# Third weight combination of a modulated four-layer convolution: 18 block products in place of 19, three of them shared

## The chip, the cores and the metric

One core of a Trainium2 chip, float32 throughout. The metric is the device time of one execution in microseconds (us). The kernel before was run three times; the profile is of one execution on the same kind of chip. Engines: PE (TensorE), DVE (VectorE), ACT (ScalarE), POOL (GpSimd), SP (DMA issue).

## The reference

128 samples, each with 64 channels of 1024 positions, go through four convolutions of three taps whose weights are modulated for each sample by a style vector; the result is added to the input.

```python
TYPES = ('same', 'upsample', 'same', 'downsample')
def _layer(x, style, w, b, mw, mb, typ):
    s = style @ mw.T + mb
    weight = SCALE * w * s[:, None, :, None]
    demod = lax.rsqrt(jnp.sum(weight * weight, axis=(2, 3)) + EPS)
    weight = weight * demod[:, :, None, None]
    if typ == 'same':         # stride 1, padding 1
        out = jax.vmap(_conv_same)(x, weight) + b[None, :, None]
    elif typ == 'upsample':   # transposed, stride 2, then blur
        out = jax.vmap(_conv_up)(x, weight.transpose(0, 2, 1, 3)) + b[None, :, None]
        out = _blur(out, 2.0 * blur_k, (1, 1))
    elif typ == 'downsample': # blur, then stride 2
        out = jax.vmap(_conv_down)(_blur(x, blur_k, (2, 2)), weight) + b[None, :, None]
    return out
return x + _L0_cond_ref(x, cond_512, ...)
```

Everything is linear, so the four layers of a sample can be merged into one filter of nine taps of 64x64, and only that filter is run over the sample.

## The kernel before

The samples are taken four at a time, in NQ = 32 groups q. PE is used as four quarters of 64x64, so that one product of a weight block with the four samples is a group of four matmuls: `r` is the row half and PSUM bank, `c` the column half. A four-byte matmul leaves two records in the trace.

**Making the filter** of a group takes four steps. `scale3` scales the last layer's weights into `wd` (ACT). `stage1_a` and `stage1_b` multiply by the third layer's weights into the PSUM tile `psS`; ACT evicts the first part as S after `stage1_a`, and `stage1_b` goes on adding into the same bank, from which DVE makes the sums (L442). `stage2` multiplies by the second layer merged with the blur (`E`) into `psR`; part of its products is shared (`share` into a free part of `psA`, `share_copy` into `psR`). ACT evicts it, scaled by `tC`, as R: seven blocks of 64 columns for each half. The **third combination**, `stage3`, multiplies R by the first layer's three taps w0, w1, w2. The filter's block j (0 to 8) is the sum over k of tap k times R block j - k. ACT evicts the nine blocks, scaled by `t0`, as `Wf`.

In the steady turns stage3 is split. `stage3_b` puts 12 blocks of products, in seven groups of matmuls, into the new group's `psA` bank: five finished filter blocks, and two products shared by two blocks each, which use sums of R blocks (`r_sums`, L588, two slots of R). ACT copies these shared ones into `psW` with the factors 1 and 1/3 (L609). `stage3_a` adds seven more blocks in four groups to `psW`, and ACT evicts four filter blocks from there. The taps j = 0, 3, 6 / 1, 4, 7 / 2, 5, 8 need the scales 1, 1/3 and -2 for what follows; they are in the weights (`w0s`), and the blocks lie in `Wf` in an order set by `TAPS`. `psS`, `psR` and `psW` share the one pair of banks of the pool `ps_w`.

**Running the filter.** Positions are split into three planes. Five products (`conv0` to `conv4`; each three groups of matmuls of 340 columns, L753) of sums of the taps (`combine_a`, `combine_b` on DVE, tile H) with sums of the planes give three outputs. DVE and POOL make the plane sums: `in_g01`, `in_g2` (tile G), `in3` (L711, DVE, into T3), `in04` (L740, DVE), and `in1` and `in2` (L726 and L731, on POOL in the steady turns). conv3, conv1, conv2 and conv0 add up in `psA`; `copy_m3` (ACT), `sum1` and `sum2` (DVE) take values out between them. `sum2` writes Y = 3 m3 - psA into the PSUM tile Y (two instructions, L662), then updates y1 (L812), and `conv4` adds its product into that Y. ACT makes the outputs (L830), SP stores them and loads the next planes.

**Order.** The schedule is written out by hand; every engine runs its instructions in the order of the program. A steady turn (`turn_of`, q = 5 to 28; q = 4 is an entry with a somewhat other order) handles output of group q, the convolutions of n = q + 1, the filter of c = q + 2 and stage1 of s = q + 4:

```python
stage2(c); conv2(q); r_sums(c, nc_g); sum2(q); in2(n, nc_g)
stage3_b(c, open_a(n)); combine_a(n); conv4(q); stage3_a(c)
combine_b(n); conv3(n); outputs(q, 2); stage1_a(s); copy_m3(n)
in04(n); share_sums(c + 1); in_g2(c); conv0(q, 0, 1, 2)
outputs(q, 1); stage1_b(s); in_g01(c); share(c + 1); share_copy(c + 1)
outputs(q, 0); conv1(n); sum1(n); in3(c); in1(c, nc_g); scale3(s + 1)
```

In q = 10, 14, 15 and 19 PE also does small matmuls for the samples' ends before conv1. Turns before q = 4 and after q = 28 use `stage3`, all 21 products.

Of the kernel before, what the change touches and what calls it, by code (L numbers as in the profile page):

```python
# [48 lines left out]
F32 = mybir.dt.float32  # L49
# [5 lines left out]
C = 64  # L55
K = 3
# [7 lines left out]
def kernel(  # L64
# [199 lines left out]
    def var_newton(bs, ls=slice(0, NL)):  # L264
# [2 lines left out]


    ALT, ODD, DOWN = slice(0, 4, 2), slice(1, 4, 2), (slice(3, 4), slice(1, 2))
    tA, tB, tBn, tC, t0, t3, td, tb = (  # L270
        const.tile([P, NQ, 2], F32, name=n) for n in ("tA", "tB", "tBn", "tC", "t0", "t3", "td", "tb")
    )

    def table(eng, t, bs, upper, lower, src, mul):
# [80 lines left out]
    Wq = {}  # L355
    chain = {}

    def scaled_copy(eng, dst, src, f):
        if eng is nc_a:
            nc_a.activation(dst, src, AF.Copy, scale=f)  # L360
        else:
            eng.tensor_scalar(dst, src, f, None, op0=ALU.mult)
# [39 lines left out]
    def flat(t):  # L402
        return t.rearrange("c a o -> c (a o)")
# [18 lines left out]
    def stage1_a(q, ps=None):  # L422

        ps = ps or unit(ps_w, f"psS{q}")
        wd = chain[q]
        tap_matmul(ps, wd, 2, 2, w2n[:, 0, :], EVEN, first=True)
        tap_matmul(ps, wd, 3, 2, w2n[:, 2, :], EVEN)
        tap_matmul(ps, wd, 1, 1, w2n[:, 1, :], slice(1, 2))
        st, t = s_tiles(q)
        for r in range(2):  # L430
            scaled_copy(nc_a, flat(st[r][:, :4]), ps[r][:, C : 5 * C], tBn[:, q, r : r + 1])
        chain[q] = wd, ps, st, t

    def stage1_b(q):

        wd, ps, st, t = chain[q]
        tap_matmul(ps, wd, 2, 1, w2n[:, 3, :], slice(3, 4))
        tap_matmul(ps, wd, 4, 1, w2n[:, 4, :], slice(4, 5), last=True)
        for r in range(2):
            p1 = st[r][:, 0:1, :].to_broadcast([P, 2, C])  # L440
            sums = ps[r][:, 2 * C : 6 * C].rearrange("c (a b o) -> c a b o", a=2, b=2)[:, :, 0]
# [43 lines left out]
    def share_copy(q):  # L485

        ps = unit(ps_w, f"psR{q}")
        for r in range(2):
            src = shared_ps[q][r].rearrange("c (a o) -> c a o", a=2)
            nc_a.copy(  # L490
                ps[r][:, C : 5 * C].rearrange("c (a b o) -> c a b o", a=2, b=2),
                src[:, :, None, :].to_broadcast([P, 2, 2, C]),
            )
        shared_ps[q] = ps

    def stage2_rest(q):

        ps = shared_ps.pop(q)
        block = lambda i, n=1: [b[:, i * C : (i + n) * C] for b in ps]
        apart = [b[:, : 4 * C].rearrange("c (a b o) -> c a b o", a=2, b=2)[:, :, 0] for b in ps]  # L500
# [16 lines left out]
        for n, (dst, weight, slots) in enumerate(plan):  # L517
            chain_matmul(dst, weight, chain[q], slots, n == len(plan) - 1)
        return ps

    def stage2(q, pool=None, engs=(nc_a, nc_a), between=None):
        st = chain[q]
        shared = q in shared_ps
        ps = stage2_rest(q) if shared else unit(pool or ps_w, f"psR{q}")
        for n, e in enumerate(() if shared else (-2, -1, 0, 1, 2, 3, 4, 5, 6)):
            if e % 2 == 0:
                a, lo, m = slice(1, 4), e // 2 + 1, 3
            else:
# [31 lines left out]

    def tap_shares():
        nc_g.tensor_sub(Wd[:, 0], woi[0][:, 0, :], woi[0][:, 1, :])
        nc_g.tensor_sub(Wd[:, 1], w0s[1][:, 2, :], w0s[1][:, 1, :])

    def blocks(ps, at):
        return [b.rearrange("c (a o) -> c a o", o=C)[:, at, :] for b in ps]
# [10 lines left out]
                    skip_group_check=True,  # L577
                )

    def stage3_out(q, ps, at, n, engs=(nc_a, nc_a)):  # L580
        W = Wq[q][0]
        for r in range(2):
            src = ps[r][:, : n * C].rearrange("c (a o) -> c a o", o=C)
            scaled_copy(engs[r], W[:, at : at + n, r], src, t0[:, q, r : r + 1])

    def r_sums(q, eng):
        t = chain[q]
        eng.tensor_add(t[:, :, 7:9], t[:, :, 2:6:3], t[:, :, 3:7:3])  # L588

    shared_w = {}  # L590

    def stage3_b(q, ps):

        new_w(q)
        t = chain[q]
        plan = (
            (slice(0, 3), w0s[2][:, 2, :], slice(0, 7, 3)),
            (slice(0, 2), w0s[2][:, 1, :], slice(1, 5, 3)),
            (slice(0, 2), w0s[2][:, 0, :], slice(2, 6, 3)),
            (slice(3, 4), w0s[0][:, 0, :], slice(0, 1)),  # L600
            (slice(4, 5), w0s[1][:, 0, :], slice(1, 2)),
            (slice(4, 5), w0s[1][:, 1, :], slice(0, 1)),
            (slice(5, 7), w0s[0][:, 1, :], slice(7, 9)),
        )
        for i, (at, weight, slots) in enumerate(plan):
            same_row(blocks(ps, at), weight, t, slots, i == 0, i == len(plan) - 1)
        pw = shared_w[q] = unit(ps_w, f"psW{q}")
        src = blocks(ps, slice(5, 7))
        for i, f in enumerate((1.0, 1.0 / 3.0)):  # L609
            for dst, v in zip(blocks(pw, slice(i, i + 3, 2)), src):  # L610
                scaled_copy(nc_a, dst, v, f)
        stage3_out(q, ps, 0, 5)

    def stage3_a(q):

        t, pw = chain[q], shared_w.pop(q)
        plan = (
            (slice(0, 3, 2), Wd[:, 0], slice(3, 7, 3)),
            (slice(0, 3, 2), w0s[0][:, 2, :], slice(1, 5, 3)),
            (slice(1, 4, 2), Wd[:, 1], slice(2, 6, 3)),  # L620
            (slice(1, 2), w0s[1][:, 0, :], slice(4, 5)),
        )
        for i, (at, weight, slots) in enumerate(plan):
            same_row(blocks(pw, at), weight, t, slots, last=i == len(plan) - 1)
        stage3_out(q, pw, 5, 4)

    def stage3(q, part, pool=None, engs=(nc_a, nc_a)):

# [6 lines left out]
        for i, kind in enumerate(kinds):  # L635
            for k in range(K):
# [610 lines left out]
    def layers(i, j):  # L1247
# [166 lines left out]
    def turn_of(q):  # L1414
# [222 lines left out]
```

## Time and profile before

| | |
|---|---|
| runs of the kernel before | 479.64, 479.15, 478.75 us; median 479.15 |
| span of the profiled execution | 478.0 us |
| granted TensorE clock, mean | 0.997 |
| DVE, 128x340 into Y (L662) | 64 instructions, mean 517 ns |
| POOL, r_sums (L588) | 24 instructions, mean 737 ns |
| POOL, in1 and in2 (L726, L731) | 28 instructions each, mean 1659 and 1660 ns |
| ACT, evictions and copies of the third combination in the steady turns | 100 of 128 columns, mean 269 ns; 50 of 320, 556 ns; 50 of 256, 470 ns |

The span runs from the first to the last instruction of one profiled execution; no other time of that execution was taken. In rows of a timeline the first number is the start in us from the span's start and the second the time from the first start to the last end of the instructions merged in the row (x2: two of them). "[0.76 <-PE psA L753]" says that the engine sat idle for 0.76 us before, until something that PE wrote to psA at line 753. In rows of groups the numbers behind the bar are busy us in all, mean ns of one, and idle us before them.

### The profile page before, as it was taken

The numbers are of one execution on the slowest core, as the hardware profiler recorded it, in microseconds if no ns is written. First come the engines' busy times: TensorE is split into PE (matmuls) and PEld (weight loads), VectorE is DVE, ScalarE is ACT, GpSimd is POOL, SyncE is SP. The second block draws the span as 40 slices with busy tenths as digits, with TensorE's granted clock in tenths as the row PEclk, the third lists the DMA queues.
The fourth block names the chain that finished last, engine by engine and source line by source line (L and its number), as shares of the span: only waits on it lengthen the run. The fifth ranks groups of instructions, "written<-read, shape, count | busy, mean of one in ns | idle before, by whom it ended". The sixth has DMA issues, their size and how long they took to land.

```text
span 478.0 us, 26721 instructions
## 1 busy us (share of the span) xinstructions
PE 469.6 (98%) x11928; PEld 346.4 (72%) x11928; DVE 417.5 (87%) x690; ACT 310.1 (65%) x708; POOL 163.5 (34%) x197
## 2 busy tenths in 40 slices
PE   8999999999999999999999999999999999999995
PEld 7877788777878876677776677766887777766652
DVE  5889998879889998899979899979989999999895
ACT  5565666667666676666667666667666768766352
POOL 3434032663335342243432233422434432333200
PEclk9999999999999999999999999999999999999998
DMA  5406365544445554345543455533455554445125
GB/s 175 158 28 200 114 195 192 150 139 144 139 150 157 173 173 127 122 151 160 171 149 120 131 170 152 173 127 126 145 169 162 162 154 146 152 146 170 61 91 191
DMA packets 50514, 70.70 MB, mean 148 GB/s; under 512 B 5664, under 2 KB 47328, under 8 KB 50400
## 3 DMA queue, kind: packets, MB, share of 16 engines
q1 hardware_dynamic: 49808, 68.32, 45.8%
q8 instruction: 93, 1.52, 1.5%
q10 hardware_dynamic: 592, 0.69, 0.5%
q14 instruction: 21, 0.17, 0.1%
HBM read 35.36 MB, written 33.62 MB: 144 GB/s over the span
## 4 chain that ended last, share of the span: by engine, by line
PE 95%; DVE 4%; issue 0%; ACT 0%; ACTq 0%; DVEq 0%
PE psA L753 45%; PE Y L753 11%; PE psR L467 9%; PE psA L571 7%; PE psW L571 7%; PE psS L389 6%; PE psR L533 4%; PE psA L467 2%; PE Y L994 2%; DVE H L662 1%; PE Y L180 1%; PE Y L336 1%; DVE G L662 0%; PE psM L204 0%; DVE o L832 0%
## 5 line engine op out<-in xcount | busy, mean ns | idle before, releaser
L753 PE MATMUL psA<-T,H 64*64 64x340 f32 x2304 | 187.3, 447 | 0.8 <-DVE y L662 0.7
L753 PEld LDWEIGHTS psA<-T,H 64*64 64x64 f32 x2304 | 89.9, 133 | 50.0 <-issue 3.1
L662 DVE SCALAR_TENSOR_TENSOR G<-X 128x1376 f32<-128x1376 f32 (+2 forms) x65 | 78.1, 1207 | 1.1 <-DMA X<-in_x 0.9
L726 POOL TENSOR_TENSOR T<-G 128x684 f32<-128x684 f32 x28 | 46.5, 1659 | 73.1 <-DVE G L662 73.1
L445 POOL TENSOR_TENSOR S<-S 128x128 f32<-128x128 f32 x28 | 22.1, 790 | 144.1 <-ACT S L360 136.8
L360 ACT ACTIVATE R<-psR,tC 128x448 f32<-128x448 f32 x63 | 36.5, 630 | 46.3 <-PE psR L467 26.7
L753 PE MATMUL psA<-T,Wf 64*64 64x340 f32 x768 | 63.9, 446 | 0.0
L753 PE MATMUL Y<-T,Wf 64*64 64x340 f32 x768 | 62.8, 451 | 0.1
L662 DVE SCALAR_TENSOR_TENSOR Y<-m,psA 128x340 f32<-128x340 f32 x64 | 33.1, 517 | 28.0 <-PE psA L753 26.6
L360 ACT ACTIVATE psW<-psA 128x128 f32<-128x128 f32 x100 | 19.3, 269 | 50.3 <-PE psA L571 46.2
L740 DVE TENSOR_TENSOR T<-G 128x1368 f32<-128x1368 f32 (+1 forms) x33 | 50.7, 1540 | 0.0
L360 ACT ACTIVATE Wf<-psW,t 128x256 f32<-128x256 f32 (+2 forms) x76 | 32.7, 479 | 26.5 <-PE psW L571 26.2
L711 DVE TENSOR_TENSOR T<-X 128x684 f32<-128x684 f32 x32 | 47.9, 1496 | 0.0
L467 PE MATMUL psR<-S,E 64*64 64x64 f32 (+1 forms) x1472 | 46.5, 238 | 0.0
L731 POOL TENSOR_TENSOR T<-G 128x684 f32<-128x684 f32 x28 | 46.5, 1660 | 0.0
L389 PEld LDWEIGHTS psS<-wd,w2n 64*64 64x64 f32 x1120 | 35.0, 133 | 13.3 <-ACT S L360 0.8
L467 PEld LDWEIGHTS psR<-S,E 64*64 64x64 f32 x1472 | 39.6, 134 | 5.2 <-ACT psR L490 0.2
L753 PEld LDWEIGHTS Y<-T,Wf 64*64 64x64 f32 x768 | 29.6, 132 | 18.0 <-DVE Y L662 0.7
L830 ACT ACTIVATE o<-psA,tb,td 128x340 f32<-128x340 f32 x63 | 37.0, 647 | 6.3 <-PE psA L753 6.3
L753 PEld LDWEIGHTS psA<-T,Wf 64*64 64x64 f32 x768 | 29.1, 133 | 15.1
L830 ACT ACTIVATE o<-Y,tb,td 128x340 f32<-128x340 f32 x63 | 36.6, 637 | 4.5 <-PE Y L753 2.7
L830 ACT ACTIVATE o<-y,tb,td 128x340 f32<-128x340 f32 x62 | 38.5, 679 | 0.6 <-DVE y L812 0.6
(165 smaller groups left out, 832.4 us busy)
## 6 DMA issues: line engine op xcount, KB each, us to landing
out<-o SPq DMA_DIRECT2D x167, 170.0 KB, 2.6
X<-in_x SPq DMA_DIRECT2D x150, 172.0 KB, 3.6
X<-in_x SPq DMA_DIRECT2D x14, 516.0 KB, 5.3
out<-o SPq DMA_DIRECT2D x6, 510.0 KB, 5.4
out<-o SPq DMA_DIRECT2D x2, 340.0 KB, 3.0
Xe<-in_x_ends SPq DMA_DIRECT2D x1, 512.0 KB, 6.7
out<-o ACTq DMA_DIRECT2D x3, 170.0 KB, 2.3
par<-in_params SPq DMA_DIRECT2D x2, 192.0 KB, 3.4
```

The source lines that it names most:

```text
L360: nc_a.activation(dst, src, AF.Copy, scale=f)
L389: nc.tensor.matmul(ps[r][cols, at * C : (at + n) * C], weight[rows], wd[c if r == 0 else 1 - c][rows, taps], start=first, stop=last, skip_ ...
L445: nc_g.tensor_add(t[:, :, 2], t[:, :, 2], t[:, :, 0])
L467: nc.tensor.matmul(dst[r][cols], weight[rows], st[c if r == 0 else 1 - c][rows, slots, :], start=False, stop=last, skip_group_check=True,)
L571: nc.tensor.matmul(dst[r][cols], weight[rows], t[rows, c, slots, :], start=first, stop=last, skip_group_check=True,)
L662: nc_v.scalar_tensor_tensor(out, x, f, y, op0=ALU.mult, op1=op)
L711: nc_v.tensor_sub(t[:, pairs, 0, :NJ], plane(X, 3, pairs), plane(X, 1, pairs))
L726: eng.tensor_add(t[:, :, 0, :NJ], plane(g, 2), plane(g, 1))
L731: eng.tensor_sub(t[:, :, 1, :NJ], plane(g, 2), plane(g, 1))
L740: nc_v.tensor_sub(t[:, pairs, :, :NJ], both(a, PL), both(b, 1))
L753: nc.tensor.matmul(ps[s][cols, :NB], w, Ts[q, tag][rows, c, i, g : g + NB], start=(g == 0 and m == 3), stop=(g == K - 1), skip_group_check ...
L830: nc_a.activation(dst, src, AF.Identity, bias=add, scale=d3)
```

## The change

The third combination is rearranged into 18 blocks of products in eight groups.

- `stage3_b` now makes six blocks in four groups: filter blocks 7 and 8 whole (three products), and three shared ones, w1 times R0+R1, R2+R3 and R4+R5. `r_sums` makes three slots of sums in place of two, and **does so on DVE in every turn** (before: on POOL, but for the entry turn).
- ACT copies each shared block twice, unscaled, into blocks 1 to 6 of `psW` (two instructions in place of four).
- `stage3_a` makes the other 12 blocks, in four groups of three, three, four and two blocks, with w0 - w1 and w2 - w1 as weights where a shared product is already there.
- The scales 1, 1/3, -2 of these seven filter blocks move from the weights into the eviction: tables `t0`, `t0b`, `t0c` (two more POOL instructions in turn 3), and two evictions of 256 columns become six, of three, two and two blocks.
- The filter lies in natural order; `psS` and `psR` move up by one block, since `psW` now needs block 0 untouched.
- In the steady turns the first third of `conv0` goes ahead of `stage1_a`, and `copy_m3` ahead of stage1_a's evictions.

On PE, around the third combination of turn q = 17, the kernel before has conv2 (psA_4979), stage3_b (psA_5249), conv4 (Y) and the start of stage3_a (psW):

```order
L753 MATMUL psA_4979<-T_17_4891,H_4694 64x340 x12
L571 MATMUL psA_5249<-R_5223,w0s_154 64x192 x4
L571 MATMUL psA_5249<-R_5223,w0s_154 64x128 x8
L571 MATMUL psA_5249<-R_5223,par 64x64 x4
L571 MATMUL psA_5249<-R_5223,w0s_153 64x64 x8
L571 MATMUL psA_5249<-R_5223,par 64x128 x4
L753 MATMUL Y<-T_17_5091,Wf_4693 64x340 x12
L571 MATMUL psW_0_5280<-R_5223,wsq 64x2x64 x2
L571 MATMUL psW_1_5281<-R_5223,wsq 64x2x64 x2
```

The changed kernel has, at the same place on PE (psA_4863 is conv2's tile, psA_5123 the new group's):

```order
L763 MATMUL psA_4863<-T_17_4775,H_4588 64x340 x12
L576 MATMUL psA_5123<-R_5097,w0s_155 64x64 x8
L576 MATMUL psA_5123<-R_5097,w0s_156 64x64 x4
L576 MATMUL psA_5123<-R_5097,par 64x192 x4
L763 MATMUL Y<-T_17_4969,Wf_4587 64x340 x12
L576 MATMUL psW_0_5142<-R_5097,wsq 64x3x64 x2
L576 MATMUL psW_1_5143<-R_5097,wsq 64x3x64 x2
```

Between conv2 and conv4 stand 16 matmuls of 6 blocks where there were 28 of 12; the wide ones are now behind conv4.

On DVE, in the same turn, before: in3 (T_18), the two halves of sum2's Y, y1, and the first of combine_a:

```order
L711 TENSOR_TENSOR T_18_5159<-X_107 128x2x342
L662 SCALAR_TENSOR_TENSOR Y<-m_17_5089,psA_4979 128x340 x2
L812 TENSOR_TENSOR y_17_5157<-y_17_5157,psA_4979 128x680
L662 SCALAR_TENSOR_TENSOR H_4981<-Wf_4980 128x384
L659 SCALAR_TENSOR_TENSOR Wf_4980<-idn_155,t_138,Wf_4980 128x64 x2
```

And on DVE after the change:

```order
L721 TENSOR_TENSOR T_18_5033<-X_107 128x2x342
L597 TENSOR_TENSOR R_5097<-R_5097 128x2x192
L672 SCALAR_TENSOR_TENSOR Y<-m_17_4946,psA_4863 128x340 x2
L822 TENSOR_TENSOR y_17_5031<-y_17_5031,psA_4863 128x680
L672 SCALAR_TENSOR_TENSOR H_4865<-Wf_4864 128x384
```

r_sums (R) has come in between in3 and sum2. On POOL the row of L588 between in1 and in2 is gone, so that in2 stands right behind in1.

On ACT, before: the shared copies into psW, the evictions to Wf, the outputs of Y, stage1_a's evictions S, and copy_m3 (m_18):

```order
L360 ACTIVATE psW_0_5280<-psA_5249 128x2x64
L360 ACTIVATE psW_1_5281<-psA_5249 128x2x64
L360 ACTIVATE psW_0_5280<-psA_5249 128x2x64
L360 ACTIVATE psW_1_5281<-psA_5249 128x2x64
L360 ACTIVATE Wf_5250<-psA_5249,t_137 128x5x64 x2
L360 ACTIVATE Wf_5250<-psW_0_5280,t_137 128x4x64
L360 ACTIVATE Wf_5250<-psW_1_5281,t_137 128x4x64
L830 ACTIVATE o_5337<-Y,tb,td 128x340 x2
L360 ACTIVATE S_5356<-psS_0_5342,tBn 128x256
L360 ACTIVATE S_5356<-psS_1_5343,tBn 128x256
L792 COPY m_18_5359<-psA_5249 128x680
```

And on ACT after the change, from the second copy on:

```order
L617 COPY psW_1_5143<-psA_5123 128x384
L365 ACTIVATE Wf_5124<-psA_5123,t_137 128x2x64 x2
L365 ACTIVATE Wf_5124<-psW_0_5142,t_137 128x3x64
L365 ACTIVATE Wf_5124<-psW_1_5143,t_137 128x3x64
L365 ACTIVATE Wf_5124<-psW_0_5142,t0b 128x2x64
L365 ACTIVATE Wf_5124<-psW_1_5143,t0b 128x2x64
L365 ACTIVATE Wf_5124<-psW_0_5142,t0c 128x2x64
L365 ACTIVATE Wf_5124<-psW_1_5143,t0c 128x2x64
L840 ACTIVATE o_5201<-Y,tb,td 128x340 x2
L802 COPY m_18_5206<-psA_5123 128x680
L365 ACTIVATE S_5226<-psS_0_5212,tBn 128x256
L365 ACTIVATE S_5226<-psS_1_5213,tBn 128x256
```

Behind stage3_a there are six evictions for two, and the m copy has passed the S evictions.

The diff, cut to its core (the shifts of psS and psR by one block are shown once):

```diff
+    def table_0_kinds():
+        for t, f in ((t0b, 1.0 / 3.0), (t0c, -2.0)):
+            nc_g.tensor_scalar_mul(t, t0, f)
...
-            scaled_copy(nc_a, flat(st[r][:, :4]), ps[r][:, C : 5 * C], tBn[:, q, r : r + 1])
+            scaled_copy(nc_a, flat(st[r][:, :4]), ps[r][:, 2 * C : 6 * C], tBn[:, q, r : r + 1])
...
-    TAPS = slice(3, 9, 2), slice(4, 9, 2), slice(0, 3)
+    TAPS = slice(0, 9, 3), slice(1, 9, 3), slice(2, 9, 3)
...
-        nc_g.tensor_sub(Wd[:, 1], w0s[1][:, 2, :], w0s[1][:, 1, :])
+        nc_g.tensor_sub(Wd[:, 1], woi[0][:, 2, :], woi[0][:, 1, :])
...
     def r_sums(q, eng):
         t = chain[q]
-        eng.tensor_add(t[:, :, 7:9], t[:, :, 2:6:3], t[:, :, 3:7:3])
+        eng.tensor_add(t[:, :, 7:10], t[:, :, 0:6:2], t[:, :, 1:7:2])
...
     def stage3_b(q, ps):
...
         plan = (
-            (slice(0, 3), w0s[2][:, 2, :], slice(0, 7, 3)),
-            (slice(0, 2), w0s[2][:, 1, :], slice(1, 5, 3)),
-            (slice(0, 2), w0s[2][:, 0, :], slice(2, 6, 3)),
-            (slice(3, 4), w0s[0][:, 0, :], slice(0, 1)),
-            (slice(4, 5), w0s[1][:, 0, :], slice(1, 2)),
-            (slice(4, 5), w0s[1][:, 1, :], slice(0, 1)),
-            (slice(5, 7), w0s[0][:, 1, :], slice(7, 9)),
+            (slice(3, 4), w0s[1][:, 2, :], slice(5, 6)),
+            (slice(3, 4), w0s[1][:, 1, :], slice(6, 7)),
+            (slice(4, 5), w0s[2][:, 2, :], slice(6, 7)),
+            (slice(0, 3), woi[0][:, 1, :], slice(7, 10)),
         )
...
-        src = blocks(ps, slice(5, 7))
-        for i, f in enumerate((1.0, 1.0 / 3.0)):
-            for dst, v in zip(blocks(pw, slice(i, i + 3, 2)), src):
-                scaled_copy(nc_a, dst, v, f)
-        stage3_out(q, ps, 0, 5)
+        for r in range(2):
+            src = ps[r][:, : K * C].rearrange("c (a o) -> c a o", o=C)
+            dst = pw[r][:, C : 7 * C].rearrange("c (a b o) -> c a b o", b=2, o=C)
+            nc_a.copy(dst, src[:, :, None, :].to_broadcast([P, K, 2, C]))
+        for r, src in enumerate(blocks(ps, slice(3, 5))):
+            scaled_copy(nc_a, Wq[q][0][:, 7:9, r], src, t0[:, q, r : r + 1])
 
     def stage3_a(q):
...
         plan = (
-            (slice(0, 3, 2), Wd[:, 0], slice(3, 7, 3)),
-            (slice(0, 3, 2), w0s[0][:, 2, :], slice(1, 5, 3)),
-            (slice(1, 4, 2), Wd[:, 1], slice(2, 6, 3)),
-            (slice(1, 2), w0s[1][:, 0, :], slice(4, 5)),
+            (slice(1, 6, 2), Wd[:, 0], slice(1, 6, 2)),
+            (slice(2, 7, 2), Wd[:, 1], slice(0, 5, 2)),
+            (slice(0, 7, 2), woi[0][:, 0, :], slice(0, 7, 2)),
+            (slice(3, 6, 2), woi[0][:, 2, :], slice(1, 4, 2)),
         )
...
-        stage3_out(q, pw, 5, 4)
+        for kind, scale in enumerate((t0, t0b, t0c)):
+            at = slice(kind, 7, K)
+            for r, src in enumerate(blocks(pw, at)):
+                scaled_copy(nc_a, Wq[q][0][:, at, r], src, scale[:, q, r : r + 1])
...
             conv2(q)
-            r_sums(c, nc_g)
+            r_sums(c, nc_v)
             sum2(q)
...
         outputs(q, 2)
+        if not entry:
+            copy_m3(n)
+            conv0(q, 0)
         if s < NQ:
             stage1_a(s)
-        if not entry:
-            copy_m3(n)
         in04(n)
...
-        conv0(q, *((2,) if entry else range(K)))
+        conv0(q, *((2,) if entry else (1, 2)))
```

More of the change, by code (lines that the diff above doesn't have):

```diff
@@ L269 @@
     ALT, ODD, DOWN = slice(0, 4, 2), slice(1, 4, 2), (slice(3, 4), slice(1, 2))
-    tA, tB, tBn, tC, t0, t3, td, tb = (
-        const.tile([P, NQ, 2], F32, name=n) for n in ("tA", "tB", "tBn", "tC", "t0", "t3", "td", "tb")
+    tA, tB, tBn, tC, t0, t0b, t0c, t3, td, tb = (
+        const.tile([P, NQ, 2], F32, name=n) for n in ("tA", "tB", "tBn", "tC", "t0", "t0b", "t0c", "t3", "td", "tb")
     )
@@ L436, in stage1_b @@
         wd, ps, st, t = chain[q]
-        tap_matmul(ps, wd, 2, 1, w2n[:, 3, :], slice(3, 4))
-        tap_matmul(ps, wd, 4, 1, w2n[:, 4, :], slice(4, 5), last=True)
+        tap_matmul(ps, wd, 3, 1, w2n[:, 3, :], slice(3, 4))
+        tap_matmul(ps, wd, 5, 1, w2n[:, 4, :], slice(4, 5), last=True)
         for r in range(2):
             p1 = st[r][:, 0:1, :].to_broadcast([P, 2, C])
-            sums = ps[r][:, 2 * C : 6 * C].rearrange("c (a b o) -> c a b o", a=2, b=2)[:, :, 0]
+            sums = ps[r][:, 3 * C : 7 * C].rearrange("c (a b o) -> c a b o", a=2, b=2)[:, :, 0]
             nc_v.scalar_tensor_tensor(
@@ L498, in stage2_rest @@
         ps = shared_ps.pop(q)
-        block = lambda i, n=1: [b[:, i * C : (i + n) * C] for b in ps]
-        apart = [b[:, : 4 * C].rearrange("c (a b o) -> c a b o", a=2, b=2)[:, :, 0] for b in ps]
+        block = lambda i, n=1: [b[:, (i + 1) * C : (i + 1 + n) * C] for b in ps]
+        apart = [b[:, C : 5 * C].rearrange("c (a b o) -> c a b o", a=2, b=2)[:, :, 0] for b in ps]
         plan = (
@@ L650, in stage3 @@
                 )
-        stage3_out(q, ps, *((3, 6), (0, 3))[part], engs)
+        stage3_out(q, ps, kinds, engs)
         return ps
```

29 lines of the change are left out of this document (16 added, 13 removed).

## The prediction

> **What bounds the kernel now.** I read the page first, then TensorE's waits, then one steady turn engine by engine.
>
> ```profile
> span 478.0 us, 26721 instructions
> PE 469.6 (98%) x11928; PEld 346.4 (72%) x11928; DVE 417.5 (87%) x690; ACT 310.1 (65%) x708; POOL 163.5 (34%) x197
> PE 95%; DVE 4%; issue 0%; ACT 0%; ACTq 0%; DVEq 0%
> PE Y L180 <- DVE eps L156: 1.4, 1, 1.4
> PE psA L571 <- issue: 0.8, 2, 0.5
> PE psA L753 <- DVE y L662: 0.7, 1, 0.7
> PE psA L753 <- DVE T L726: 0.2, 1, 0.2
> ```
>
> The busy times and the chain of work say the same: TensorE (PE) is busy for 98% of the span and is 95% of the chain. The last four rows are all its waits, 3.1 us together. No wait is left that a shorter PE program could run into for free, and any wait that the change makes is added to the time in full. So I follow one steady turn (q = 17) on PE. The columns are start, duration, what, and how many records (a four-byte matmul leaves two).
>
> ```profile
> 277.38 1.90 PE L753 MATMUL psA<-T,H 64*64 64x340 f32 x24
> 279.09 0.94 PE L571 MATMUL psA<-R,w0s 64*64 64x192 f32 x24
> ...
> 280.20 0.40 PE L571 MATMUL psA<-R,par 64*64 64x128 f32 x8
> 280.46 1.95 PE L753 MATMUL Y<-T,Wf 64*64 64x340 f32 x24
> 282.23 0.40 PE L571 MATMUL psW<-R,wsq 64*64 64x128 f32 x8
> ...
> 283.00 1.90 PE L753 MATMUL psA<-T,H 64*64 64x340 f32 x24
> 284.71 0.73 PE L389 MATMUL psS<-wd,w2n 64*64 64x128 f32 x24
> 285.26 1.90 PE L753 MATMUL psA<-T,Wf 64*64 64x340 f32 x24
> 286.98 0.41 PE L389 MATMUL psS<-wd,w2n 64*64 64x64 f32 x16
> ...
> 291.22 0.47 PE L753 MATMUL psA<-T,H 64*64 64x340 f32 x4
> ```
>
> From start to start: conv2 1.71 us, stage3_b 1.37, conv4 1.77, stage3_a 0.77, conv3 1.71, stage1_a 0.55, conv0 1.72, stage1_b 0.23, then share, conv1 and stage2 until the next conv2: a turn of 13.84 us. One group of four matmuls takes time by its columns: conv2 has three groups of 340 columns in 1.71 us, so a block of 64 columns costs 0.107 us. stage3_b (12 blocks) comes to 0.114 per block, stage3_a (7 blocks) to 0.110. I use 0.11.
>
> Now the other engines in the same turn. From here on times are counted from conv2's start, 277.38.
>
> ```profile
> 276.70 1.87 DVE L711 TENSOR_TENSOR T<-X 128x684 f32<-128x684 f32 x1
> 279.34 1.07 DVE L662 SCALAR_TENSOR_TENSOR Y<-m,psA 128x340 f32<-128x340 f32 x2 [0.76 <-PE psA L753]
> 280.32 0.85 DVE L812 TENSOR_TENSOR y<-y,psA 128x680 f32<-128x680 f32 x1
> 281.09 0.57 DVE L662 SCALAR_TENSOR_TENSOR H<-Wf 128x384 f32<-128x384 f32 x1
> ```
>
> VectorE's sum2 waits for conv2's end (1.71) and writes Y from 1.96 to 3.03. conv4 adds into Y, and it starts at 3.08, 0.05 later. stage3_b's last group began at 280.20 and holds two blocks, so PE came free at about 280.42, or 3.04. **stage3_b is exactly the work that covers sum2**; the slack there is some 0.04 us.
>
> **The change part by part.**
>
> (1) PE work. Per turn 19 blocks in 11 groups become 18 in 8. That is 0.11 us less, in 25 turns 2.8 us.
>
> (2) The split. stage3_b goes from 12 blocks to 6, so PE would be at conv4 at 1.71 + 0.66 = 2.37. Y is not there before 3.08, so the 0.66 us taken out ahead of conv4 turn into a wait. stage3_a goes from 7 blocks to 12, behind conv4: 5 x 0.11 = +0.55 us. Moving this work costs **+0.55 us in each turn**, where the count of blocks alone promises -0.11.
>
> (3) r_sums. It grows from two slots of R to three and goes from POOL (GpSimd) to VectorE, ahead of sum2. What it meets there:
>
> ```profile
> 276.18 1.67 POOL L726 TENSOR_TENSOR T<-G 128x684 f32<-128x684 f32 x1 [2.81 <-DVE G L662]
> 278.91 0.73 POOL L588 TENSOR_TENSOR R<-R 128x256 f32<-128x256 f32 x1 [1.06 <-ACT R L360]
> 279.59 1.66 POOL L731 TENSOR_TENSOR T<-G 128x684 f32<-128x684 f32 x1
> ```
>
> ```profile
> 277.67 1.16 ACT L360 ACTIVATE R<-psR,tC 128x448 f32<-128x448 f32 x2 [0.73 <-PE psR L467]
> ```
>
> R is evicted at 1.45 and r_sums could start on VectorE at 1.53, as it does now on POOL. For its 128x384 the nearest row is the 128x384 of L662 above, 0.57 us. Undisturbed it ends at 2.1 and delays sum2 by about 0.05. But it stood between POOL's in1 (L726) and in2 (L731), and held in2 back until 2.2. With it gone nothing holds in2, and it follows in1 at once. Two rows show what in1 does to VectorE's in3 (L711). In the turn above, in3 started 0.52 us into in1 and took 1.87 us, ending 0.72 after it. In a turn where in1 was over, it took 0.86:
>
> ```profile
> 260.68 1.65 POOL L726 TENSOR_TENSOR T<-G 128x684 f32<-128x684 f32 x1 [2.77 <-DVE G L662]
> 262.71 0.86 DVE L711 TENSOR_TENSOR T<-X 128x684 f32<-128x684 f32 x1
> L711 DVE TENSOR_TENSOR T<-X x32: 857/1800/2172, 14.0 to 456.6; 128x684 f32<-128x684 f32 x32
> ```
>
> The last row has in3's shortest, median and longest, in ns: most are held. So in3 does not slow down beside in1, it waits for nearly all of it (all but the last 0.14 us). sum2, with one operand in PSUM, ran beside in2 at 279.59 and was not held. r_sums reads R twice from SBUF, as in3 does with X. After the change in2 starts when in3 lets go, at 1.19 - 0.14 = 1.05, and ends at 2.71. r_sums, asked for at 1.53, gets through at 2.57 and ends at 3.14. sum2 follows from about 3.05 to 4.12, and conv4 starts at 4.17 in place of 3.08: +1.09. If in2 goes ahead of the waiting in3 it ends at 2.13, in3 at 2.85, r_sums at 3.33, conv4 at 4.36: +1.28. A longer turn gives VectorE slack, so that G and in1 come earlier against conv2, which takes some of it back. The ends are +0.05 and +1.28; I take **+0.80**, nearer to the row that shows the blocking. In four turns (after the ends' matmuls of q = 10, 14, 15 and 19, as at 262.71) in1 is over before in3 asks, and in2 will be too: +0.05 there.
>
> The Trainium skill has a rule on this, in "SBUF — State Buffer", section "Who interferes with whom": a VectorE instruction with two SBUF inputs contends with a GpSimd instruction that reads SBUF, and the later one is blocked for the whole instruction. By it r_sums would go at 2.71 and the step would be 0.14 dearer; the rows of in3 agree with the blocking, and have the handover 0.14 us before the end. No sum here uses the rule.
>
> (4) ScalarE (ACT). Copies into psW: four of 128 columns (0.77 us) become two of 384, and the tap evictions behind them shrink; done some 1.5 us behind stage3_b, they lie under conv4's wait and run. Behind stage3_a two evictions become six, and copy_m3 now goes ahead of the S evictions.
>
> ```profile
> 280.73 0.77 ACT L360 ACTIVATE psW<-psA 128x128 f32<-128x128 f32 x4 [1.90 <-PE psA L571]
> ...
> 283.27 0.84 ACT L360 ACTIVATE Wf<-psW,t 128x256 f32<-128x256 f32 x2 [0.93 <-PE psW L571]
> 284.00 1.16 ACT L830 ACTIVATE o<-Y,tb,td 128x340 f32<-128x340 f32 x2
> 285.48 0.84 ACT L360 ACTIVATE S<-psS,tBn 128x256 f32<-128x256 f32 x2 [0.32 <-PE psS L389]
> 286.21 0.72 ACT L792 COPY m<-psA 128x680 f32<-128x680 f32 x1
> 286.81 1.25 ACT L830 ACTIVATE o<-y,tb,td 128x340 f32<-128x340 f32 x2
> L360 ACT ACTIVATE Wf<-psW,t 128x256 f32<-128x256 f32 x50 | 21.0, 470 | 22.0 <-PE psW L571 22.0
> L360 ACT ACTIVATE Wf<-psW,t 128x192 f32<-128x192 f32 x13 | 4.8, 418 | 0.4 <-PE psW L571 0.3 <-PE Y L914 0.2
> L360 ACT ACTIVATE psW<-psA 128x128 f32<-128x128 f32 x100 | 19.3, 269 | 50.3 <-PE psA L571 46.2 <-issue 4.1
> ```
>
> ACT starts 0.27 us behind PE (283.00 to 283.27) and its instructions overlap by 0.1: an eviction of 256 columns occupies 0.365, an output 0.52, the m copy 0.60. 192 columns are 0.052 shorter (418 against 470 ns), so 0.31; 128 columns by the same slope 0.26. From stage3_a's end: 0.27 + 2 x 0.31 + 4 x 0.26 + 2 x 0.52 + 0.60 + 0.365 + 0.47 = 4.41 until the second S eviction is through, and stage1_b adds into the bank that it reads. PE is there after conv3 1.71, a third of conv0 0.57, stage1_a 0.55 and the rest of conv0 1.15 = 3.98. With 0.05 for the signal PE waits **0.48 us**. (Now the S evictions end at 286.32, 0.66 ahead of stage1_b at 286.98.) The bounds are 0.2 with the 0.19 of the psW copies for each of the four small ones, and 0.67 with the 0.31 of 192 columns. The two new tables on POOL lie in turn 3, where no wait on POOL shows; nothing on SP's queue moves.
>
> The sum. Turns of this kind are q = 4 to 28, 25 by the 100 psW copies. q = 4 has no conv2 in it: I put it at +0.4, for its S eviction. 20 turns x (0.80 + 0.55) = 27.0; 4 x (0.05 + 0.55) = 2.4; the S wait in 23 turns (stage1_a ends at q = 27) x 0.48 = 11.0; with 0.4, +40.8 us. The profiled span of 478.0 becomes 518.8; the median of the runs, 479.15, lies 1.15 above the span, so **520.0 us**.
>
> **The rivals.**
> - No collision: r_sums is not held by in2, as if in2 were late or long done. 24 x 0.60 + 11.0 + 0.4 = +25.8, **505**. For it: r_sums needs only 0.57 us and VectorE stood idle for 0.76 there. Against: in3, of the same form, is held in nearly every turn. Chance 0.22.
> - Collision, but no S wait (small evictions at 0.19 or less, or PE later for another reason): +29.4, **508.6**. Chance 0.11. Neither of the two: +14.4, **493.6**. Chance 0.09.
> - The other side: only PE's work counts, and 18 products for 19 give -2.8, **476.4**. Its place is conv4's start; it decides if Y is complete by 2.37, when PE would be there. Today it is complete at 3.03, 1.3 us after conv2's end, of which 1.07 is sum2 itself. Nothing in the change shortens that. Chance 0.03.
> - Dearer than forecast: in2 ahead of in3 in all 24 turns and small evictions at 0.31, 24 x (1.28 + 0.55) + 23 x 0.67 + 0.6 = +60, **539**. Chance 0.05.
>
> **How the numbers follow.** The forecast, 520, has 0.50. The range 494 to 530 takes in the first two rivals and the forecast with the spread of its terms, and leaves out about 0.16. About 0.2% (1 us) is what a measurement of this kernel can tell from no change. Faster by more than that 0.03, within it 0.01, slower 0.96: even the mildest mix of (2) alone is 13 us.
>
> **What would show it.** In the changed profile PE should wait for VectorE's Y ahead of conv4 by 0.7 us or more in all 24 turns, and its share fall towards 91%; stage3_b and stage3_a should take 0.66 and 1.32 us without waits. r_sums on VectorE should take about 1.6 us where in2 runs beside it, 0.57 in the four turns after the ends' matmuls; if it takes 0.57 everywhere, the collision is wrong. PE should wait for ACT's S ahead of stage1_b's matmuls by about 0.5; no such wait means my price of the small evictions is wrong. The forecast falls altogether if conv4 starts within 2.5 us of conv2.

## The result and the profile after

| | us |
|---|---|
| before, median of 4 runs | 479.25 (478.75 to 479.64) |
| changed, median of 4 runs | 521.79 (521.22 to 523.92) |
| ratio changed to before | 1.0899, 95% interval 1.0874 to 1.0924 |
| changed, the profiled execution: time and span | 521.32 and 519.5 |

The change makes the kernel 9% slower; 520.0 was forecast. The page of the changed kernel, the lines that answer to those of before:

```profile
span 519.5 us, 25591 instructions
PE 488.4 (94%) x11328; PEld 359.6 (69%) x11328; DVE 444.9 (86%) x714; ACT 324.0 (62%) x758; POOL 149.7 (29%) x175
PE 59%; DVE 13%; ACT 4%; issue 4%; DMA 0%; ACTq 0%; DVEq 0%
PE psA L763 26%; PE Y L763 10%; PE psR L472 8%; PE psW L576 7%; PE psS L394 5%; DVE R L597 5%; DVE Y L672 5%; ACT R L365 3%; PE Y L1004 2%; PE psA L472 1%; ACT o L840 1%; DVE T L721 1%; DVE G L672 1%; ACT Wf L365 1%; PE psR L538 0%
```

PE was 95% of the chain of work; now it is 59%, and r_sums (DVE R) and sum2 (DVE Y) stand in it with 5% each. There are 1200 matmul and weight-load records fewer (12 matmuls of two records in 25 turns are 600 of each kind), so the work did shrink. PE's busy time rose all the same, from 469.6 to 488.4 us, since a wait inside a run of matmuls can be counted as busy (that for S, below, is one); the time is in waits. For 3.4 us of turn q = 14 (252.58 to 255.99) the granted TensorE clock of this execution was 0.50, and conv4 and stage3_a together took 1.7 us longer there than in the other turns (2.97 and 1.78 us in place of 1.77 and 1.30).

The waits of PE and of its weight loads (PEld), as total us, how often, and the longest:

```profile
PE psA L576 <- DVE R L597: 12.4, 20, 1.3
PE Y L763 <- DVE Y L672: 10.4, 24, 0.5
PEld Y L763 <- DVE Y L672: 19.5, 25, 0.8
PEld psS L394 <- ACT S L365: 17.3, 48, 0.6
PEld psA L576 <- DVE R L597: 15.1, 20, 1.4
L597 DVE TENSOR_TENSOR R<-R x25: 552/1361/1985, 93.2 to 474.6; 128x384 f32<-128x384 f32 x25
```

There are three producers, and none of them held PE's matmuls before (the page before has S holding the weight loads for 0.8 us in all): r_sums in 20 turns, Y in 24, the S evictions in 48 matmuls (two banks, 24 turns). The last row has the shortest, median and longest r_sums in ns: 0.55 us where nothing is in its way, 1.36 in the middle.

The turn of q = 17 on PE:

```profile
298.65 0.45 PE L763 MATMUL psA<-T,H 64*64 64x340 f32 x2
...
301.60 0.56 PE L576 MATMUL psA<-R,par 64*64 64x192 f32 x8 [0.62 <-DVE R L597]
302.58 1.95 PE L763 MATMUL Y<-T,Wf 64*64 64x340 f32 x24 [0.42 <-DVE Y L672]
304.34 0.83 PE L576 MATMUL psW<-R,wsq 64*64 64x192 f32 x16
...
305.64 1.90 PE L763 MATMUL psA<-T,H 64*64 64x340 f32 x24
...
308.48 1.33 PE L763 MATMUL psA<-T,Wf 64*64 64x340 f32 x16
309.77 0.75 PE L394 MATMUL psS<-wd,w2n 64*64 64x64 f32 x14
...
310.67 0.45 PE L763 MATMUL psA<-T,H 64*64 64x340 f32 x2
...
314.32 0.46 PE L763 MATMUL psA<-T,H 64*64 64x340 f32 x2
```

From conv2 to conv2 15.67 us in place of 13.84. conv4 starts 3.93 us after conv2 (before: 3.08), stage3_a takes 1.30 (0.77), and from its end to conv1 it is 5.03 (4.56). These three differences, 0.85, 0.53 and 0.47, come to 1.85, and the rest of the turn gives 0.02 back.

DVE and POOL around r_sums in that turn:

```profile
297.81 1.82 DVE L721 TENSOR_TENSOR T<-X 128x684 f32<-128x684 f32 x1
300.13 1.42 DVE L597 TENSOR_TENSOR R<-R 128x384 f32<-128x384 f32 x1 [0.50 <-ACT R L365]
301.47 1.05 DVE L672 SCALAR_TENSOR_TENSOR Y<-m,psA 128x340 f32<-128x340 f32 x2
297.24 1.66 POOL L736 TENSOR_TENSOR T<-G 128x684 f32<-128x684 f32 x1 [2.29 <-DVE G L672]
298.87 2.27 POOL L741 TENSOR_TENSOR T<-G 128x684 f32<-128x684 f32 x1
```

The last two rows are in1 and in2. in3 (L721) waits for in1 and ends 0.73 after it; in2 takes 2.27 in place of 1.65, since it waits for in3; r_sums, asked for at 300.13, waits for in2 (until 301.14) and ends 0.41 after it; only then does sum2 run. It is a relay: in1 holds in3, in3 holds in2, and in2 holds r_sums.

ACT behind stage3_a in the same turn:

```profile
305.92 0.73 ACT L365 ACTIVATE Wf<-psW,t 128x192 f32<-128x192 f32 x2 [2.25 <-PE psW L576]
306.54 0.62 ACT L365 ACTIVATE Wf<-psW,t0b 128x128 f32<-128x128 f32 x2
307.04 0.64 ACT L365 ACTIVATE Wf<-psW,t0c 128x128 f32<-128x128 f32 x2
307.54 1.19 ACT L840 ACTIVATE o<-Y,tb,td 128x340 f32<-128x340 f32 x2
308.57 0.77 ACT L802 COPY m<-psA 128x680 f32<-128x680 f32 x1
309.18 0.91 ACT L365 ACTIVATE S<-psS,tBn 128x256 f32<-128x256 f32 x2
```

ACT works without a gap from 305.92 to the end of S at 310.09, 4.45 us after stage3_a's end. stage1_b's first matmul is there at 309.77, and its two blocks, 0.23 us of work, take until share begins past 310.3. PE had come there by about 309.62, since conv0's last two thirds, begun at 308.48, take 1.15. This wait is hidden in PE's busy time; the row of PEld shows it.

### The profile page after: what moved, and what is told of

Read it like the earlier page. It is cut to its first block, busy times and chain, and to the rows that moved or that the text cites. A ratio compares the mean times of both kernels' runs of the same rounds, so it can differ in the third digit from the quotient of the medians.

```text
span 519.5 us, 25591 instructions
## 1 busy us (share of the span) xinstructions
PE 488.4 (94%) x11328; PEld 359.6 (69%) x11328; DVE 444.9 (86%) x714; ACT 324.0 (62%) x758; POOL 149.7 (29%) x175
## 4 chain that ended last, share of the span: by engine, by line
PE 59%; DVE 13%; ACT 4%; issue 4%; DMA 0%; ACTq 0%; DVEq 0%
PE psA L763 26%; PE Y L763 10%; PE psR L472 8%; PE psW L576 7%; PE psS L394 5%; DVE R L597 5%; DVE Y L672 5%; ACT R L365 3%; PE Y L1004 2%; PE psA L472 1%; ACT o L840 1%; DVE T L721 1%; DVE G L672 1%; ACT Wf L365 1%; PE psR L538 0%
## 5 line engine op out<-in xcount | busy, mean ns | idle before, releaser
L763 PEld LDWEIGHTS psA<-T,H 64*64 64x64 f32 x2304 | 106.5, 133 | 36.3 <-issue 2.0
L450 POOL TENSOR_TENSOR S<-S 128x128 f32<-128x128 f32 x28 | 12.8, 458 | 236.8 <-ACT S L365 229.5
L763 PE MATMUL Y<-T,Wf 64*64 64x340 f32 x768 | 63.7, 460 | 10.5 <-DVE Y L672 10.4
L365 ACT ACTIVATE Wf<-psW,t 128x192 f32<-128x192 f32 (+1 forms) x76 | 30.0, 444 | 62.0 <-PE psW L576 61.7
L365 ACT ACTIVATE R<-psR,tC 128x448 f32<-128x448 f32 x63 | 36.5, 630 | 47.5 <-PE psR L472 30.3
L736 POOL TENSOR_TENSOR T<-G 128x684 f32<-128x684 f32 x28 | 46.5, 1660 | 67.8 <-DVE G L672 61.0
L741 POOL TENSOR_TENSOR T<-G 128x684 f32<-128x684 f32 x28 | 59.0, 2107 | 0.0
L394 PEld LDWEIGHTS psS<-wd,w2n 64*64 64x64 f32 x1120 | 37.0, 132 | 23.7 <-ACT S L365 17.3
L617 ACT COPY psW<-psA 128x384 f32<-128x384 f32 x50 | 21.2, 468 | 50.3 <-PE psA L576 46.0
L472 PE MATMUL psR<-S,E 64*64 64x64 f32 (+1 forms) x1472 | 51.4, 238 | 0.1
L472 PEld LDWEIGHTS psR<-S,E 64*64 64x64 f32 x1472 | 47.4, 134 | 2.7 <-issue 0.5
L721 DVE TENSOR_TENSOR T<-X 128x684 f32<-128x684 f32 x32 | 49.2, 1536 | 0.0
L394 PE MATMUL psS<-wd,w2n 64*64 64x64 f32 (+1 forms) x1120 | 41.4, 245 | 0.8
L597 DVE TENSOR_TENSOR R<-R 128x384 f32<-128x384 f32 x25 | 29.5, 1181 | 14.1 <-ACT R L365 14.1
L447 DVE SCALAR_TENSOR_TENSOR S<-psS,tB,S 128x128 f32<-128x128 f32 x56 | 17.1, 346 | 28.5 <-PE psS L394 15.4
```

Of the source, the lines that this page charges most:

```text
L394: nc.tensor.matmul(ps[r][cols, at * C : (at + n) * C], weight[rows], wd[c if r == 0 else 1 - c][rows, taps], start=first, stop=last, skip_ ...
L472: nc.tensor.matmul(dst[r][cols], weight[rows], st[c if r == 0 else 1 - c][rows, slots, :], start=False, stop=last, skip_group_check=True,)
L597: eng.tensor_add(t[:, :, 7:10], t[:, :, 0:6:2], t[:, :, 1:7:2])
L721: nc_v.tensor_sub(t[:, pairs, 0, :NJ], plane(X, 3, pairs), plane(X, 1, pairs))
L736: eng.tensor_add(t[:, :, 0, :NJ], plane(g, 2), plane(g, 1))
L741: eng.tensor_sub(t[:, :, 1, :NJ], plane(g, 2), plane(g, 1))
```

## The experiments

Each is one edit, and each was compared with runs of the kernel before on the same chip. In the first four that kernel took 479.54 us, in the next four 480.55, in the last two 479.67 us. Where kernels of different groups are compared, it is by what each lies above its own group's kernel before; the changed kernel lies 42.5 us above (521.79 - 479.25).

**r_sums on POOL again** (x1_sums_pool), in the changed kernel:

```diff
-            r_sums(c, nc_v)
+            r_sums(c, nc_g)
```

> The changed kernel with r_sums back on POOL, between in1 and in2; three slots as in the change. Theory (three terms: the split, the collision of r_sums with in2, the S evictions): only the collision goes. On POOL r_sums takes some 1.0 us (between 0.73 for 256 columns and 1.65 for 684), ends 2.5 us after conv2's start, ahead of sum2's end, so conv4 starts at 3.1 again. Removed: 0.80 x 20 + 0.05 x 4 = 16 us, time about 505, and PE waits for Y by about 0.7 in each turn. Rival (r_sums is not held by in2, VectorE is late for another reason, and the split and S cost more than I put): within 3 us of the changed kernel, 519 to 522.

Measured 505.52 us, ratio 1.0544 (1.0517 to 1.0571): 26.0 us above the kernel before, 16.5 less than the changed kernel.

```profile
L597 POOL TENSOR_TENSOR R<-R x24: 993/997/1089, 107.3 to 459.9; 128x384 f32<-128x384 f32 x24
```

On POOL it takes 1.0 us, as estimated, and nearly all of it is covered by the wait for sum2: in one turn conv4 starts 3.16 us after conv2 (305.66 and 308.82). PE's wait is not where I expected it, though: it waits for R, 6.1 us in 22 turns, and only 0.5 us for Y. That takes the collision away, but also r_sums' place on DVE; the next run separates the two.

**r_sums on DVE, in2 held behind it** (x2_gate):

```diff
+    gate = const.tile([P, 1], F32, name="gate")
...
             r_sums(c, nc_v)
+            nc_g.tensor_copy(gate, chain[c][:, 0, 9, :1])
             sum2(q)
```

> The changed kernel with r_sums on VectorE, and one POOL copy of a single column of its result ahead of in2, so that in2 cannot run beside r_sums. Theory (the held-back r_sums is the collision with in2): r_sums takes 0.55 us in every turn, conv4 starts 3.1 to 3.2 us after conv2, time 503 to 507. Rival (it is r_sums' place on VectorE ahead of sum2 that costs, not in2): r_sums stays at 1.2 to 1.6 us and the time at 519 to 522.

Measured 505.58 us, 1.0546 (1.0511 to 1.0581), the same as with r_sums on POOL. Its timeline, one turn (L598 is r_sums, L1437 the added copy, L742 in2, the other L673 the first of combine_a):

```profile
306.60 0.56 DVE L598 TENSOR_TENSOR R<-R 128x384 f32<-128x384 f32 x1 [0.33 <-ACT R L366]
307.13 1.07 DVE L673 SCALAR_TENSOR_TENSOR Y<-m,psA 128x340 f32<-128x340 f32 x2
308.88 0.83 DVE L673 SCALAR_TENSOR_TENSOR H<-Wf 128x384 f32<-128x384 f32 x1
307.29 0.18 POOL L1437 COPY gate<-R 128x1 f32<-128x1 f32 x1 [1.75 <-DVE R L598]
307.65 1.65 POOL L742 TENSOR_TENSOR T<-G 128x684 f32<-128x684 f32 x1 [0.17 <-issue]
L598 DVE TENSOR_TENSOR R<-R x25: 546/558/614, 93.8 to 459.6; 128x384 f32<-128x384 f32 x25
```

With in2 behind it, r_sums takes 0.56 us in every turn. DVE has the same instructions in the same order as in the changed kernel, so the 16.5 us are the collision with in2, not the move to DVE. conv4 starts 3.16 us after conv2 in this turn (305.09 and 308.25), as with r_sums on POOL. sum2 runs beside in2 and is not held; combine_a's L673, with both operands in SBUF, is (0.83 in place of 0.55).

**copy_m3 behind the S evictions** (x3_s_first), in the changed kernel:

```diff
         if not entry:
-            copy_m3(n)
             conv0(q, 0)
         if s < NQ:
             stage1_a(s)
+        if not entry:
+            copy_m3(n)
```

> The changed kernel with copy_m3 put behind the S evictions again; the first third of conv0 stays ahead of stage1_a. Theory (stage1_b waits for S because ACT is busy with six evictions, two outputs and the m copy): S is through at about 3.9 us after stage3_a's end in place of 4.4, PE arrives at 4.0, the wait of 0.48 in 23 turns goes: 511. Rival (the 0.5 us between conv0 and share are PE's own, not a wait for S): no change, 520 to 522. Rival 2 (the m copy, later now, delays sum1 or the psR copies): a new wait in their place, 515 or more.

Measured 509.46 us, 1.0625 (1.0597 to 1.0654): 29.9 us above, 12.6 us less than the changed kernel, against 11 expected.

```profile
PEld psS L394 <- ACT S L365: 0.4, 2, 0.2
```

Of the 17.3 us that PEld waited for S, 0.4 are left. Not all of the gain is that wait. In one turn the stretch from stage3_a's end to conv1 is 4.71 us (299.71 to 304.42), against 5.03 in the changed kernel and 4.56 before, so 0.15 stay; what holds conv1 for them is not shown (copy_m3, now later, ends 0.14 ahead of it, at 304.28). And r_sums takes 1.23 us at the median in place of 1.36, so that conv4 starts 3.75 us after conv2 in that turn in place of 3.93: the repair eases the collision too. Summed over the turns q = 5 to 28 of the two profiled executions, the first stretch gives 8.2 us and conv4's start 2.2.

**Both** (x4_pool_s_first):

> The changed kernel with both: r_sums on POOL and copy_m3 behind the S evictions. Theory: what is left is the split alone, 24 turns x 0.55 = 13 us over the kernel before, about 493, a turn of about 14.4 us, PE waiting for Y by 0.7 us in each turn. Rival (18 products for 19 is a gain once the order is mended): 476 to 479.

Measured 493.05 us, 1.0281 (1.0256 to 1.0306), the time that the theory had. With both repairs the change is still 13.5 us slower than the kernel before. Its turn:

```profile
284.32 1.90 PE L763 MATMUL psA<-T,H 64*64 64x340 f32 x24
...
286.90 0.56 PE L576 MATMUL psA<-R,par 64*64 64x192 f32 x8
287.40 1.95 PE L763 MATMUL Y<-T,Wf 64*64 64x340 f32 x24
289.17 0.83 PE L576 MATMUL psW<-R,wsq 64*64 64x192 f32 x16
...
290.47 0.47 PE L763 MATMUL psA<-T,H 64*64 64x340 f32 x4
```

conv4 starts 3.08 us after conv2, to the hundredth where it started before, with half of stage3_b's blocks gone; stage3_a takes 1.30 us. The 0.7 us ahead of conv4 that the theory had are not there: the wait lies ahead of the shared group (286.90; 6.4 us in 19 turns for POOL's r_sums) more than ahead of conv4 (0.3 us in all for Y).

**r_sums on DVE in the kernel before** (x5_before_sums_dve), two slots, nothing else:

```diff
-            r_sums(c, nc_g)
+            r_sums(c, nc_v)
```

> The kernel before with one part of the change alone: r_sums (two slots) on VectorE. Theory (collision with in2, whatever the products): r_sums takes some 1.3 to 1.6 us in about 20 turns in place of 0.46, conv4 starts 0.7 to 1.0 us later there: 493 to 499. Rival (the collision needs the changed kernel's longer turn, or in2 loses to VectorE): 479 to 481.

Measured 497.49 us, 1.0359 (1.0339 to 1.0379), 17 us slower.

```profile
L588 DVE TENSOR_TENSOR R<-R x25: 418/1396/1859, 93.4 to 450.7; 128x256 f32<-128x256 f32 x25
285.05 2.29 POOL L731 TENSOR_TENSOR T<-G 128x684 f32<-128x684 f32 x1
PE Y L753 <- DVE Y L662: 10.1, 20, 0.5
```

One word in the kernel before brings the collision: the 0.42 us instruction takes 1.4 at the median, in2 is held by in3 (2.29), and conv4 waits for sum2 behind it (10.1 us in 20 turns). The collision needs neither the 18 products nor a longer turn.

**The change's order in the kernel before** (x6_before_order):

```diff
+        if not entry:
+            copy_m3(n)
+            conv0(q, 0)
         if s < NQ:
             stage1_a(s)
-        if not entry:
-            copy_m3(n)
...
-        conv0(q, *((2,) if entry else range(K)))
+        conv0(q, *((2,) if entry else (1, 2)))
```

> The kernel before with the change's order alone: copy_m3 ahead of the S evictions, the first third of conv0 ahead of stage1_a. Theory (the S wait comes of the six evictions and the order together): with two evictions of 256 columns S is through 3.9 us after stage3_a's end, PE arrives at 4.0: no change, 478 to 481. Rival (the order by itself makes stage1_b wait): 0.3 us or more in 23 turns, 486 or more.

Measured 480.54 us, 1.0005 (0.9993 to 1.0017): nothing. The order costs only together with the six evictions.

**The order of before in the changed kernel** (x8_old_order), the same lines the other way:

> The changed kernel with the order of before around stage1_a: conv0 unsplit behind stage1_a, copy_m3 behind the S evictions. Theory: stage1_a comes 0.57 us earlier and waits for the evictions from psW, through at 2.07 us after stage3_a's end where PE comes at 1.71: 0.36 to 0.4 us in place of 0.48, time 518 to 521. Rival (the change's order hides the evictions): slower than the changed kernel by 5 us or more.

Measured 517.03 us, 1.0765 (1.0745 to 1.0785), 36.5 above, 6.0 us less than the changed kernel; about 2 were expected (518 to 521): a miss.

```profile
PEld psS L394 <- ACT Wf L365: 12.8, 24, 0.5
303.88 1.90 PE L763 MATMUL psA<-T,H 64*64 64x340 f32 x24
305.72 0.91 PE L394 MATMUL psS<-wd,w2n 64*64 64x128 f32 x20
308.71 0.46 PE L763 MATMUL psA<-T,H 64*64 64x340 f32 x1
```

The wait is where I expected it (stage1_a for the evictions from psW). But stage1_a starts its first bank 1.84 us behind stage3_a, where conv3 is through at 1.71, since it needs only the first half of the evictions for that. conv1 starts 4.83 us after stage3_a here and 5.03 in the changed kernel (310.67), 0.20 less, which is 4.6 us in 23 turns. Part of that goes again at conv4, which starts 1.7 us later in the sum of the turns: the spans of the two profiled executions lie only 3.3 us apart (516.2 and 519.5). The rest of the 6.0 comes with the comparison across groups, whose kernels before differ by 1.3 us, and the spread of the runs. The change's order is the dearer one for its own evictions; the size of my estimate was off.

**Idle work in the wait** (x7_pad): x4_pool_s_first with six blocks of products more at the end of stage3_b, which nothing reads.

```diff
             same_row(blocks(ps, at), weight, t, slots, i == 0, i == len(plan) - 1)
+        for i in range(2):
+            same_row(blocks(ps, slice(5, 8)), woi[0][:, 0, :], t, slice(0, 3))
```

> The kernel with r_sums on POOL and copy_m3 behind the S evictions, plus six blocks of idle products (two groups of matmuls of three blocks each into unused blocks of psA, never read) at the end of stage3_b. Theory (the six blocks taken out of stage3_b are a wait for sum2 now): the idle products lie in that wait, same time as without them within 2 us, about 493. Rival (PE is not waiting for Y there, its own work sets conv4): 25 turns x 0.66 = +16 us, about 509.

Measured 504.82 us, 1.0507 (1.0489 to 1.0524), 24.3 above, 10.8 us more than without: a miss, nearer to the rival.

```profile
290.04 1.90 PE L765 MATMUL psA<-T,H 64*64 64x340 f32 x24
...
292.63 1.21 PE L576 MATMUL psA<-R,par 64*64 64x192 f32 x24 [0.34 <-POOL R L597]
293.65 1.90 PE L765 MATMUL Y<-T,Wf 64*64 64x340 f32 x24
```

The idle products stand behind the shared group, and that one waits for POOL's r_sums until 2.59 us after conv2. So most of the slack lies ahead of it, and the idle work pushes conv4 to 3.61 us after conv2. The expectation had put the whole slack behind r_sums. With r_sums early the test is clean:

**The same idle work with r_sums at 2.1 us** (x9_gate_pad): x2_gate with the same two lines.

> The kernel with the one-column POOL copy ahead of in2 (r_sums ends 2.1 us after conv2's start there, where POOL's r_sums ended at 2.55), plus the same six blocks of idle products at the end of stage3_b. Theory (they lie in the wait for sum2, once r_sums is early): stage3_b ends at 3.1 with them, Y is there at 3.1, so within 2 us of the kernel without them, 505 to 508. Rival (the +12 us that the idle products cost with r_sums on POOL are their price anywhere): 516 to 519.

Measured 506.66 us, 1.0562 (1.0546 to 1.0578), 27.0 above, 1.0 us more than x2_gate.

```profile
306.93 0.46 PE L766 MATMUL psA<-T,H 64*64 64x340 f32 x2
310.09 1.95 PE L766 MATMUL Y<-T,Wf 64*64 64x340 f32 x24
```

conv4 starts 3.16 us after conv2, with the six blocks as without them in x2_gate. At 0.66 us in each of 25 turns they would cost 16.5 us if they were paid; here they are as good as free. They are as many as the change took out of stage3_b.

**One block moved back** (x10_block0): x4_pool_s_first with filter block 0 in stage3_b.

```diff
+            (slice(5, 6), woi[0][:, 0, :], slice(0, 1)),
             (slice(0, 3), woi[0][:, 1, :], slice(7, 10)),
...
-            (slice(0, 7, 2), woi[0][:, 0, :], slice(0, 7, 2)),
+            (slice(2, 7, 2), woi[0][:, 0, :], slice(2, 7, 2)),
...
+        for r, src in enumerate(blocks(ps, slice(5, 6))):
+            scaled_copy(nc_a, Wq[q][0][:, 0:1, r], src, t0[:, q, r : r + 1])
...
-            at = slice(kind, 7, K)
+            at = slice(kind or K, 7, K)
```

> The kernel with r_sums on POOL and copy_m3 behind the S evictions (493.05), with filter block 0, one product, made in stage3_b ahead of the shared group and not in stage3_a, and evicted from psA. Theory (work ahead of conv4 is hidden, work behind it is paid, 0.11 us a block): 24 x 0.11 = 2.6 us less, 490 to 491. Rival (only the number of blocks counts): no change, 493.

Measured 490.58 us, 1.0224 (1.0206 to 1.0242): 10.9 above, 2.6 us less than x4_pool_s_first, 0.11 us a turn. In one turn conv4 starts 3.09 us after conv2 (282.96 and 286.05), as without the block, and stage3_a takes 1.19 us (287.82 to 289.01) in place of 1.30. It is the fastest form of the 18 products that was tried, and 2.2% slower than the kernel before.

## Why the prediction was right

The forecast of 520.0 rested on three terms and a small one for the entry turn. The first two were taken out, each by itself and both together; the third is what was left then. The last column sums the rows of the profiled executions before and after over the turns q = 5 to 28.

| term | forecast, us | measured by taking it out, us | by the rows, us |
|---|---|---|---|
| the collision of r_sums with in2 | 20 x 0.80 + 4 x 0.05 = 16.2 | 16.5 (x1), 16.5 (x2) | 15.3 (conv4 later behind conv2) |
| the S evictions behind ACT's queue | 11.0 | 12.6 (x3) | 10.4 (conv1 later behind stage3_a) |
| the split: work moved behind conv4 | 24 x 0.55 = 13.2 | 13.5 left in x4 | 12.7 (stage3_a, 24 x 0.53) |
| the entry turn | 0.4 | not tried alone | |
| sum | 40.8 | 42.6, against 42.5 in all | 38.4, of 41.5 between the spans |

- **What bounds the kernel.** With no wait left on PE, each new wait showed in full. The first two terms add up: 16.5 and 12.6 taken out singly, 29.0 together. Of the 3.1 us that the rows leave over, 1.7 are the stretch at half clock in turn 14; the rest is spread over the start and single turns.
- **The split.** conv4's start stayed at 3.08 us with half the blocks ahead of it (x4); idle work of the same size in their place was as good as free (x9), and a block moved back saved its 0.11 us (x10). Fewer products lost because PE's time ahead of conv4 was not on the path, while that behind it was.
- **The collision.** The order came as the first case had it: in3 gets through ahead of the waiting in2, and r_sums waits for in2. conv4 at 3.93 was forecast as 3.88. That r_sums goes undisturbed in the four turns after the ends' matmuls was right too: PE waits for R in 20 turns of 24, and in the other four conv4 starts at 3.15 to 3.18.
- **What was luck.** The worked case gave conv4 at 4.17, +1.09; the 0.80 was picked between that and 0.05, with a reason for the direction (in1 comes earlier against conv2) but no row for the size. In turn 17 in1 starts 1.41 us ahead of conv2 in place of 1.20, r_sums is through at 2.90 in place of 3.14, and conv4 comes 0.24 earlier than worked out. That the pick was right to 0.05 us is luck.
- **The rule of the Trainium skill** in "SBUF — State Buffer", section "Who interferes with whom", has the same blocking. Taken for the whole of both instructions it would have made a turn 0.14 us dearer, an estimated 2.8 us in 20. The rows agree with the blocking and speak for the shorter wait: r_sums ends 0.41 us after in2 though it takes 0.56 alone. Whether in2 lets go 0.15 us before its end, or r_sums has that much of its work behind it while it waits, they do not tell apart.
- **ACT.** S was through 4.45 us after stage3_a's end; 4.41 was forecast. The 12.6 of x3 are not a better measure of this term than the rows, since x3 eased the collision too. The price of the small evictions, 0.26 us each, stands in the rows as about 0.25 (306.54 to 307.54 for four).
- **What was off.** I expected PE to wait for Y by 0.7 us or more in each turn, and its busy share to fall towards 91%. PE's row shows 0.42, since 0.62 of the wait was taken by the shared group waiting for r_sums just before; and the share is 94%, since busy time holds part of the waits: of the 18.8 us that it grew, 9.3 went when x3 took out the wait for S (488.4 to 479.1). r_sums was to take about 1.6 us beside in2 and took 1.36 at the median.
- **The rivals.** "Only PE's work counts", 476.4, falls with x4 and x10. The three milder ones, 505, 508.6 and 493.6, fell by the waits that they left out: the first two by one each, the third by both. As forecasts of the kernel without those waits they came out well: 505.5, 509.5 and 493.1. The dearer one, 539, needed in2 ahead of in3 in every turn and 0.31 us for a small eviction; in3 went first in the turn shown, and the evictions took about 0.25.

## What to carry to other kernels

When one engine is busy all the time, ask of each piece of work if it covers a wait: a block taken out ahead of one saves nothing, and if it is moved behind, it is paid in full. Before an instruction changes engine, look at what it held back on the old one, and whether that now runs beside it and holds it up. Splitting one eviction into three lengthens the queue in front of whatever comes next on that engine; order that queue by who is waited for first.

## What the runs showed of the hardware

- The DVE instructions with two operands in SBUF and the POOL tensor additions here exclude each other in both directions: in2 took 2.27 us in place of 1.65 behind in3, r_sums 1.42 in place of 0.56 behind in2. The DVE instructions with one operand in PSUM (sum2, 1.07 us for two) ran beside in2 without loss.
- The one that waited got through ahead of the next instruction in the other engine's queue: in3 came between in1 and in2, though in2 stood right behind in1.
- A small ACT eviction into SBUF scaled from a table took longer than a copy from PSUM to PSUM scaled by a number: 372 to 388 ns for 128 columns in the changed kernel's groups below, against 269 for the copies into psW of the kernel before. The two differ in target and scale, and which of them costs was not tried.

```profile
L365 ACT ACTIVATE Wf<-psW,t0c 128x128 f32<-128x128 f32 x50 | 16.0, 388 | 0.0
L365 ACT ACTIVATE Wf<-psW,t0b 128x128 f32<-128x128 f32 x50 | 15.7, 372 | 0.0
```
